# A 3x3 convolution by minimal filtering, and the opening of a scan stage written out for all engines by halves

## The chip, the cores and the metric

The kernel runs on one core of one Trainium2 chip, all in fp32. The metric is the time on the device in microseconds (us). A core has five engines with an instruction queue each: TensorE (PE in the profile; PEld is its weight load), VectorE (DVE), ScalarE (ACT), GpSimd (POOL) and SyncE (SP, which here only issues transfers). An engine works through its own queue in order; between engines, semaphores say when a result is there.

## The reference, cut to what matters

Four layers, each added onto x, each behind a group norm (32 groups of 4 channels); x is 2 images of 128 channels and 56 x 56 points.

```python
# layer 0: agent attention;  layer 1: 3x3 convolution;  layer 2: experts on 2x2 patches;  layer 3: two mambas
x = x + _L0_conv_ref(_gn(x), ...)
x = x + _L1_conv_ref(_gn(x), L1_conv_weight, L1_conv_bias)
x = x + _L2_conv_ref(_gn(x), L2_conv_router_w, L2_conv_w1, L2_conv_w2)
x = x + _L3_conv_ref(_gn(x), ...)

def _L1_conv_ref(x, weight, bias):      # pad 1, stride 1, by FFT in the reference
    ...
    return out + bias[None, :, None, None]

def _mamba(x, in_w, conv_w, conv_b, xproj_w, dt_w, dt_b, Alog, Dp, out_w):
    xi, z = jnp.split(x @ in_w.T, 2, axis=-1)
    xc = jax.nn.silu(conv_b + sum((xp[:, k:k + L, :] * conv_w[:, k] for k in range(K))))
    dt, Bm, Cm = jnp.split(xc @ xproj_w.T, [DT_RANK, DT_RANK + D_STATE], axis=-1)
    dt = jax.nn.softplus(dt @ dt_w.T + dt_b)
    # per row of the image, along its 56 points:
    h = jnp.exp(dt_l[:, :, None] * A) * h + (dt_l * u_l)[:, :, None] * B_l[:, None, :]
    y = jnp.einsum('bds,bs->bd', h, C_l)
    ...
```

The second mamba runs over reversed rows; both results are fused, normalized and added onto x.

## The kernel before, in words

x stays on the chip, channels on partitions (`net.x`, [128, 2, 3136]). An image is worked in seven blocks of 448 points (8 rows of 56). `net.xb(b, k)` is block k of image b, `net.take_stats` its bn_stats; `net.norm_stages` gives the group norm in three stages (bn_aggr; a matmul for group means; a matmul and an inverse root for deviations).

**Attention** (`short_attention`). Fourteen blocks (7 per image), each of 25 steps over the keys. In a step TensorE makes scores (line 617), ScalarE their exponentials (620), VectorE adds them up (`ex_sum`, 625 and 627), and TensorE multiplies by values (635). The order of PE, ScalarE and VectorE is written out (`manual_schedule`), and other work is put into the steps one stage at a time: for the block before (`after`), for the next block (`ahead`), and from a list, `rest`. The denominators (`sum_up`, 655) need VectorE's sums. From the last but one block on, `rest` holds the norm of image 0 for the convolution and its seven `conv.pad` stages: a memset of the edges on GpSimd and a norm on VectorE (line 135) into a padded image of 58 x 58, in the room of `xn0`.

**Convolution** (`Conv3x3`). `loads` brings the weights and transposes the nine taps. `block` makes a block of 8 rows by nine matmuls of 448 columns (line 910), one for each tap, on shifted views of the padded image; one VectorE instruction adds result and bias onto x (917), another takes statistics. Image 0's seven blocks follow the attention, with the seven last stages of the last attention block between them (`tail`). Then comes a verdict over the softmaxes' ranges (`worst`, `bad`, `w_ps`, 830 to 848), the last use of the attention's memory. Image 1 (`convolved(1)`) is done inside `experts.route`: its norm, its pads, its seven blocks; after two of them come the patches of image 0 (`patches(0)`: norm, four normalized quarters, router logits, transposes into DRAM). This part is ordered by the scheduler of the framework. The weights of the mambas (`MambaWeights`) are loaded from ScalarE's queue in the same stretch.

**Experts.** Routing sorts tokens into tiles; 28 tiles run two matmul layers each, with weights streamed by SyncE.

**Mambas** (`mamba_pair`). `arrive(b)` fetches the experts' rows by 14 gathers on GpSimd (`combine`, two for each of seven pieces; line 1200), adds each pair on VectorE (1311), transposes on TensorE (1315), adds onto x (1321), takes statistics, and then the norm of image b. An image block then goes through two halves (ways), f and b. Of a half: `conv` (two matmul groups, m = 0 and 1), `silu` (which loads a ScalarE table for Silu and then the one for exp and log), `low` and `send_low` (projections, through DRAM to B and C), `step`/`error`/`log`/`softplus` (dt, with m = 0 and 1), `weigh` (dt x xc on GpSimd, line 1673, and a memset in dt) and `send_steps` (eight transfers that spread dt and dtu, line 1686, by SyncE). Then 16 units of the scan: `decay` (ScalarE, 1700), `push` (GpSimd, 1711), `scan` (VectorE, 1733), multiplication by C on GpSimd (1739) or VectorE (1742), `collect` (TensorE). There are 28 halves and 448 units.

The order of the scans is written out for all engines: `book(step, stage)` puts a stage at a step of an agenda, 32 steps a block; its `fetch`, which reads the PSUM result, runs a step later. The first block's stages have negative steps. In the opening only ScalarE's order is written out; the others follow the scheduler, and `arrive(1)` comes after the negative steps in the program.

Of the kernel before, what the change touches and what calls it, by code (L numbers as in the profile page):

```python
# [166 lines left out]
def agent_attention(net, wide=None, conv=None):  # L167
# [5 lines left out]
    with ExitStack() as ctx:  # L173
# [48 lines left out]
        def queries(b):  # L222
# [28 lines left out]
            for k in range(NBLK):  # L251
                et = work.tile([2 * agents, 2, BLK], F32, name="et", tag="et", bufs=1)
                e_ps = sc_ps.tile([P, 2, 512], F32, name="e_ps", tag="sc")
                for half in range(2):
# [16 lines left out]
                    en = work.tile(shape, F32, name="a_en", tag="a_en")  # L271
# [137 lines left out]
def short_attention(net, wide, conv):  # L409
# [20 lines left out]
    with ExitStack() as ctx:  # L430
# [35 lines left out]
        taps = conv.loads(one.tile([P, N], F32, name="cw", tag="k1")[:, : 9 * P], bank)  # L466
# [5 lines left out]
        for b in range(NB):  # L472
# [3 lines left out]
            m.va = one.tile([P, len(tiles), P], F32, name=f"va{b}")  # L476
# [59 lines left out]
        def keys(m, k):  # L536
            if k == 0:
                m.k = one.tile([P, N], F32, name=f"k{m.b}", tag=f"k{m.b}")
            cols = slice(k * BLK, (k + 1) * BLK)
            k_ps = bank("k_ps")  # L540
            nc.tensor.matmul(k_ps[:, :BLK], wk, m.xn[:, cols], start=True, stop=True)
            return lambda: nc.scalar.copy(m.k[:, cols], k_ps[:, :BLK])
# [225 lines left out]
        with tc.manual_schedule(engines={E.PE, E.Activation, E.DVE}):  # L768
# [10 lines left out]
            for n, blk in enumerate(blocks):  # L779
                if n == len(blocks) - 2:  # L780
                    pad = one.tile([P, PAD * PAD], F32, name="pad0", tag="xn0")
                    rest = conv.norm(0, banks, "mm")
                    rest += [lambda k=k: conv.pad(0, pad, k) for k in range(NBLK)]
# [36 lines left out]
            tail = [getattr(prev, after[i]) for i in sorted(after)]  # L820
            for k in range(NBLK):
                if k < len(tail) and tail[k]:
                    fetch = tail[k]()
                conv.block(0, k, pad, bank("conv_ps"))
                if k < len(tail) and tail[k] and fetch:
                    fetch()
# [28 lines left out]
class Conv3x3:  # L855


    def __init__(self, net, keep):
        self.net = net
        self.wt = keep.tile([P, 9, P], F32, name="cwt")  # L860
        self.bias = net.column("L1_conv_bias")
        self.norms = {}

    def loads(self, raw, bank):
# [5 lines left out]
        def turn(some):  # L870
            ps = bank("cw_ps")
            for n, k in enumerate(some):
                nc.tensor.transpose(ps[:, n * P : (n + 1) * P], w[:, :, k], net.ident)
            to = self.wt[:, some[0] : some[-1] + 1, :].rearrange("c k f -> c (k f)")
            return lambda: nc.scalar.copy(to, ps[:, : len(some) * P])

        return [lambda some=some: turn(some) for some in (range(0, 4), range(4, 8), range(8, 9))]
# [9 lines left out]
    def pad(self, b, pad, k):  # L887

        nc = self.net.nc
        p3 = pad.rearrange("c (h w) -> c h w", w=PAD)  # L890
        r0 = 1 + k * ROWS
        edges = [p3[:, r0 : r0 + ROWS, 0], p3[:, r0 : r0 + ROWS, PAD - 1]]
        if k == 0:
            edges.append(p3[:, 0, :])
        if k == NBLK - 1:
            edges.append(p3[:, PAD - 1, :])
        for edge in edges:
            nc.gpsimd.memset(edge, 0.0)
        self.net.normed(
            p3[:, r0 : r0 + ROWS, 1 : PAD - 1],  # L900
            self.net.xb(b, k).rearrange("c (h w) -> c h w", w=HW),
            self.norms[b],
        )

    def block(self, b, k, pad, acc):
        net, nc = self.net, self.net.nc
        p3 = pad.rearrange("c (h w) -> c h w", w=PAD)
        for n in range(9):
            i, j = divmod(n, 3)
            nc.tensor.matmul(  # L910
                acc[:, :BLK].rearrange("f (r w) -> f r w", w=HW),
                self.wt[:, n, :],
                p3[:, k * ROWS + i : k * ROWS + i + ROWS, j : j + HW],
                start=n == 0,
                stop=n == 8,
            )
        nc.vector.scalar_tensor_tensor(net.xb(b, k), acc[:, :BLK], self.bias, net.xb(b, k), ALU.add, ALU.add)
        net.take_stats(b, k)
# [6 lines left out]
class PatchExperts:  # L925
# [15 lines left out]
    def route(self, dram, wpool, conv):  # L941
# [9 lines left out]
        with tc.tile_pool(name="l2_route", bufs=1) as one, tc.tile_pool(  # L951
# [116 lines left out]
            for k, _ in enumerate(conv(1)):  # L1068
                if k == 1:
# [230 lines left out]
    def combine(self, b, gathered, bank):  # L1300

        net, nc = self.net, self.net.nc
        half = self.half
        for k in range(self.nt // NB):
# [7 lines left out]

# [5 lines left out]
            r0 = k * (T // half)  # L1318
            for q in range(4):
                xv = self.place(b, q)[:, r0 : r0 + T // half, :]  # L1320
                nc.vector.tensor_tensor(
                    xv, xv, tp[:, q * T : (q + 1) * T].rearrange("c (h w) -> c h w", w=half), ALU.add
                )
            net.take_stats(b, k)
# [102 lines left out]
def mamba_pair(net, out, wts, combine):  # L1427
# [19 lines left out]
    with ExitStack() as ctx:  # L1447
# [20 lines left out]
        def arrive(b):  # L1468

            combine(b, gathered, wide_bank)  # L1470
            mean, rstd = net.group_norm(b, ps, "mm")
# [3 lines left out]
            norms[b] = (both_of[:, 1:2], both_of[:, 0:1])  # L1475

# [96 lines left out]
        class Half:  # L1573
# [97 lines left out]
            def weigh(self):  # L1671
                self.dtu = self.u
                nc.gpsimd.tensor_mul(self.dtu, self.dt, self.xc)

                at = 0 if self.w.d == "f" else HW - 1
                nc.gpsimd.memset(self.dt.rearrange("p m (r t) -> p (m r) t", t=HW)[:, :, at : at + 1], 1e31)

            def send_steps(self, first=False):

                self.dt2 = work.tile([P, 2, 2, BLK], F32, name="dt2", tag="dt2")  # L1680
                self.dtu2 = work.tile([P, 2, 2, BLK], F32, name="dtu2", tag="dtu2")
                for some in (slice(0, 1), slice(1, 2)) if first else (slice(0, 2),):
# [303 lines left out]
```

## Time and profile before

| | us |
|---|---|
| median of three timed runs | 3152.46 (3149.33 to 3153.22) |
| the profiled execution, its own time | 3161.96 |
| its span in the trace | 3160.2 |
| TensorE, VectorE, ScalarE, GpSimd busy | 2864.5, 2200.8, 1752.5, 1411.3 |
| conv 0: first matmul | 884.9 |
| conv 1: first matmul, last eviction | 946.8, 1002.0 |
| first expert matmul | 1050.1 |
| first gather, first scan of the mambas | 1697.6, 1786.25 |

In a row of the timeline: start (us), length (us), engine, line, operation, out<-in with shapes, how many were merged, and in brackets the engine's idle time before it with what ended it. "remote" is a wait whose releaser the trace does not show, "issue" time in which the engine waited for nothing shown. A matmul in fp32 leaves two records, and the ends of matmuls are modelled. Windows give busy time of each engine in a stretch and the granted TensorE clock (1.00 is full).

### The profile page before, as it was taken

How to read it: one execution, taken by the hardware profiler on the slowest of the kernel's cores; microseconds unless marked ns; L12 is line 12 of the kernel's file. 1: busy time of each engine (PE TensorE's matmuls, PEld its weight loads, DVE VectorE, ACT ScalarE, POOL GpSimd, SP SyncE). 2: the span in 40 equal slices, each digit the busy share in tenths (PEclk: the TensorE clock that was granted, in tenths of full speed). 3: DMA queues.
4: the chain of work that ended last, by engine and by line, in shares of the span. 5: the costliest groups of instructions: out<-in, count | busy, mean ns of one | idle time of the engine just before them, and what ended most of it. 6: DMA issues, size and time to landing. Idle time of an engine off the chain costs nothing. (4 is left out here: it accounts for less than half of the span.)

```text
span 3160.2 us, 34597 instructions
## 1 busy us (share of the span) xinstructions
PE 2864.5 (91%) x13024; PEld 1091.8 (35%) x13024; DVE 2200.8 (70%) x1985; ACT 1752.5 (55%) x2618; POOL 1411.3 (45%) x755
## 2 busy tenths in 40 slices
PE   7999999999998899999985689898999899898985
PEld 3333333333344444444442223333233333233321
DVE  5879989988954111111112479999999999999996
ACT  5777887887811011111110467767777767777764
POOL 2000100100000000000003389999999999999995
PEclk9999999999999899999996789998899988999987
DMA  1000000000011878787755434444444444444450
GB/s 53 1 1 1 1 1 1 1 1 1 1 37 41 319 285 319 287 318 287 318 200 165 90 80 86 103 89 102 91 88 90 98 95 95 91 86 99 85 107 7
DMA packets 133525, 333.65 MB, mean 106 GB/s; under 512 B 20228, under 2 KB 90724, under 8 KB 129748
## 3 DMA queue, kind: packets, MB, share of 16 engines
q1 hardware_dynamic: 111744, 304.88, 33.6%
q0 software_dynamic: 5136, 14.70, 1.4%
q10 hardware_dynamic: 16452, 11.61, 1.1%
q8 instruction: 107, 1.75, 0.2%
q14 instruction: 86, 0.70, 0.1%
HBM read 262.56 MB, written 17.20 MB: 89 GB/s over the span
## 5 line engine op out<-in xcount | busy, mean ns | idle before, releaser
L1711 POOL TENSOR_TENSOR dBu<-dtu,Bs 128x896 f32<-128x896 f32 x448 | 923.8, 2090 | 76.1 <-DVE h L1733 60.7
L1733 DVE TENSOR_TENSOR_SCAN h<-dA,dBu 128x896 f32<-128x896 f32 x448 | 878.8, 2007 | 57.5 <-ACT dA L1700 57.2
L620 ACT ACTIVATE ex<-sc 128x896 f32<-128x896 f32 (+1 forms) x700 | 602.7, 917 | 114.0 <-PE sc L617 102.5
L627 DVE TENSOR_TENSOR ex_sum<-ex_sum,ex 128x1792 f32<-128x1792 f32 (+1 forms) x238 | 489.7, 2057 | 35.8 <-ACT ex L620 21.7
L1753 PE MATMUL y<-h,both 128*64 128x448 f32 x1792 | 474.4, 631 | 15.5 <-POOL h L1739 12.9
L617 PE MATMUL sc<-q,k 32*128 32x448 f32 (+1 forms) x2800 | 402.5, 586 | 3.6 <-ACT ex L620 2.9
L1249 PE MATMUL h_ps<-w,xs_c 128*128 128x512 f32 x896 | 392.1, 596 | 10.7 <-issue 9.9
L1700 ACT ACTIVATE dA<-dt,f_A 128x448 f32<-128x448 f32 x448 | 284.5, 637 | 108.9 <-DVE h L1733 76.1
L635 PE MATMUL av<-ex,va 128*32 128x448 f32 (+1 forms) x2800 | 334.3, 552 | 0.1
L1742 DVE TENSOR_TENSOR h<-h,c_ps 128x1792 f32<-128x1792 f32 x154 | 311.3, 2022 | 31.1 <-PE c_ps L1721 16.2
L582 POOL TENSOR_TENSOR a_e<-a_e,a_inv 112x784 f32<-112x784 f32 x14 | 41.6, 2974 | 625.6 <-ACT ex L620 437.2
L1700 ACT ACTIVATE dA<-dt,b_A 128x448 f32<-128x448 f32 x448 | 283.7, 636 | 63.3 <-DVE h L1733 50.4
L1253 DVE TENSOR_TENSOR he<-h_ps,sg 128x512 f32<-128x512 f32 x56 | 38.6, 692 | 397.4 <-PE h_ps L1249 375.0
L1200 POOL DMA_INDIRECT xr<-xd,whom x28 | 28.2, 1005 | 592.7 <-PE xr_ps L1239 489.2
L1739 POOL TENSOR_TENSOR h<-h,Cs 128x1792 f32<-128x1792 f32 x70 | 279.2, 3988 | 2.4 <-DVE h L1733 1.9
L1721 PE MATMUL c_ps<-low,ident 40*64 40x448 f32 x616 | 175.9, 653 | 89.8 <-DVE h L1742 67.6
L1249 PEld LDWEIGHTS h_ps<-w,xs_c 128*128 128x128 f32 x896 | 168.6, 191 | 218.7 <-issue 202.0
L1753 PEld LDWEIGHTS y<-h,both 128*64 128x64 f32 x1792 | 117.9, 152 | 322.6 <-issue 252.9
L617 PEld LDWEIGHTS sc<-q,k 32*128 32x128 f32 (+1 forms) x2800 | 137.7, 181 | 228.8 <-issue 129.5
L1270 PE MATMUL o_ps<-w,ht 128*128 128x512 f32 x448 | 200.0, 599 | 8.0 <-DMA w<-in_L_conv_w_dram 8.0
L1272 ACT ACTIVATE ot<-o_ps,share 128x512 f32<-128x512 f32 x28 | 19.3, 688 | 287.1 <-PE o_ps L1270 287.1
L1252 ACT ACTIVATE sg<-h_ps 128x512 f32<-128x512 f32 x56 | 33.4, 597 | 257.4 <-PE h_ps L1249 257.3
(318 smaller groups left out, 3007.3 us busy)
## 6 DMA issues: line engine op xcount, KB each, us to landing
w<-in_L_conv_w_dram SPq DMA_DIRECT2D x28, 4096.0 KB, 19.4
w<-in_L_conv_w_dram SPq DMA_DIRECT2D x28, 2048.0 KB, 10.2
Bs<-far SPq DMA_DIRECT2D x56, 896.0 KB, 10.5
dtu<-sp_u SPq DMA_DIRECT2D x108, 224.0 KB, 3.9
dt<-dt SPq DMA_DIRECT2D x108, 224.0 KB, 5.2
Cs<-far SPq DMA_DIRECT2D x140, 112.0 KB, 7.4
os<-ot ACTq DMA_DIRECT2D x28, 256.0 KB, 7.8
xd<-xt SPq DMA_DIRECT2D x14, 224.0 KB, 2.7
```

Of the source, the lines that this page charges most:

```text
L617: nc.tensor.matmul(sc[:size, j, :BLK], self.m.k[rows, at : at + size], self.q[rows, :], start=True, stop=True)
L620: nc.scalar.activation(ex[:size, 2 * g : 2 * g + 2, :], sc[:size, :, :BLK], AF.Exp, scale=scale)
L627: nc.vector.tensor_add(self.total[g][:size], self.total[g][:size], ex[:size])
L635: nc.tensor.matmul(self.av[rows, :BLK], self.m.va[:size, i, rows], self.ex[i][:size, h, :], start=i == 0, stop=i == STEPS - 1,)
L1249: nc.tensor.matmul(h_ps, xc[:, q, :], w1[:, q, f0 : f0 + 512], start=q == 0, stop=q == 3)
L1270: nc.tensor.matmul(o_ps, ht[:, i, :], w2[:, i, :], start=i == 0, stop=i == nj - 1)
L1700: nc.scalar.activation(self.dA[u][:, r * BLK : (r + 1) * BLK], self.dt2[:, m, r, :], AF.Exp, scale=self.w.A[:, j, 2 * m + r : 2 * m + r + 1],)
L1711: nc.gpsimd.tensor_tensor(self.dBu[u], self.dtu2[:, m], self.B[:, j, :].unsqueeze(1).to_broadcast(shape), ALU.mult)
L1733: nc.vector.tensor_tensor_scan(hf, af, bf, 0.0, ALU.mult, ALU.add)
L1739: nc.gpsimd.tensor_tensor(h4, h4, c, ALU.mult)
L1742: nc.vector.tensor_tensor(h4, h4, c, ALU.mult)
L1753: nc.tensor.matmul(self.y[r * H : (r + 1) * H, m, :BLK], both, self.hc[j][:, m, r, :], start=False, stop=j == PAIRS - 1)
```

## The change

1. The convolution is done by minimal filtering along the rows, F(2,3): each pair of neighbouring outputs comes from four products (planes) instead of six. The taps k0, k1, k2 of a row become k0, (k0+k1+k2)/2, (k0-k1+k2)/2, k2, made by four GpSimd operations (`mix`). The input becomes four planes of half width, made by four tensor_tensors for each block: on GpSimd for image 0, on VectorE for image 1 (`planes`). The work goes by groups of 16 rows (the last of 8), in two parts, left and right: two planes of three matmuls each. Results are put together from PSUM by VectorE and ScalarE, and by two GpSimd operations (`group`, `rest`).
2. The tail of the attention becomes eight parts with the remaining stages and the three stages of image 1's norm between them. `patches(0)` comes after the first group of image 1 instead of its second block.
3. `combine` and `arrive` become generators: the transposed piece is added onto x one piece later. All five engines' order in the opening is written out: `arrive(0)`, and then the negative steps with pieces of `arrive(1)` between them. `seen`, a small ScalarE copy, stands ahead of the table load.
4. In the first block both convs of a half are booked side by side in two PSUM banks, f's dt is made, weighed (on VectorE) and sent by halves, and dt goes out from ScalarE's queue, dtu from SyncE's. b's convs are booked behind this.

```diff
@@ short_attention
-                    pad = one.tile([P, PAD * PAD], F32, name="pad0", tag="xn0")
+                    planes = [
...
+                        for i, tag in enumerate(("xn0", "k0"))
+                    ]
+                    scratch = one.tile([P, len(tiles), P], F32, name="scratch", tag="va0")
...
-                    rest += [lambda k=k: conv.pad(0, pad, k) for k in range(NBLK)]
+                    rest += [lambda k=k: conv.planes(0, planes, k, scratch, nc.gpsimd) for k in range(NBLK)]
...
+            total, means, deviations = conv.norm(1, banks, "mm")
+            tail = [
+                [prev.divide],
+                [prev.project, prev.measure, prev.root],
+                [prev.normalize],
+                [prev.turn_back, prev.restat, total],
+                [means],
+                [deviations],
+            ]
...
+            for n, (part, ready) in enumerate(parts):
+                for stage in tail[n] if n < len(tail) else ():
+                    do(stage)
+                part()
+                if ready:
+                    ready()
+            end()
@@ class Conv3x3
+    GROUPS = ((0, 16), (16, 16), (32, 16), (48, 8))
...
+    def planes(self, b, planes, k, scratch, engine):
...
+        at = k % 2 * ROWS * PAD
+        p3 = scratch[:, at : at + ROWS * PAD].rearrange("c (h w) -> c h w", w=PAD)
+        nc.gpsimd.memset(p3[:, :, :: PAD - 1], 0.0)
         self.net.normed(
+            p3[:, :, 1 : PAD - 1], self.net.xb(b, k).rearrange("c (h w) -> c h w", w=HW), self.norms[b]
         )
+        even, odd = (p3.rearrange("c h (w two) -> c h two w", two=2)[:, :, i, :] for i in range(2))
...
+                (even[:, :, :half], even[:, :, 1:], ALU.subtract),
+                (odd[:, :, :half], even[:, :, 1:], ALU.add),
+                (even[:, :, 1:], odd[:, :, :half], ALU.subtract),
+                (odd[:, :, :half], odd[:, :, 1:], ALU.subtract),
...
+            engine.tensor_tensor(planes[n // 2][:, n % 2, rows, :], left, right, op)
...
+        def products(two):
+            m = banks("conv_ps")
+            for i in range(2):
+                for row in range(3):
+                    nc.tensor.matmul(
+                        m[:, i, :n],
+                        self.wt[:, row, 2 * two + i, :],
+                        planes[two][:, i, r0 + row : r0 + row + rows, :].rearrange("c h w -> c (h w)"),
...
+        def left():
+            m = products(0)
+            nc.vector.tensor_tensor(x[:, 0], x[:, 0], grid(m[:, 0, :n]), ALU.add)
+            nc.scalar.activation(first, m[:, 1, :n], AF.Identity, bias=self.bias, scale=1.0)
+
+        def right():
+            m = products(1)
+            nc.scalar.copy(second, m[:, 0, :n])
+            nc.vector.tensor_tensor(x[:, 1], x[:, 1], grid(m[:, 1, :n]), ALU.subtract)
+
+        def rest():
+            nc.gpsimd.tensor_tensor(gap, first, second, ALU.subtract)
+            nc.gpsimd.tensor_tensor(first, first, second, ALU.add)
+
+            nc.vector.tensor_tensor(x[:, 1], x[:, 1], grid(gap), ALU.add)
+            nc.vector.tensor_tensor(x[:, 0], x[:, 0], grid(first), ALU.add)
+            for k in range(r0 // ROWS, (r0 + rows) // ROWS):
+                net.take_stats(b, k)
@@ mamba_pair
+            def weigh(self, m=None):
...
+                engine = nc.gpsimd if m is None else nc.vector
+                engine.tensor_mul(self.dtu[:, some], self.dt[:, some], self.xc[:, some])
...
+            def send_steps(self, m=None):
...
+                for to, src, queue in ((self.dtu2, self.dtu, nc.sync), (self.dt2, self.dt, nc.sync if m is None else nc.scalar)):
...
+                book(at + 3, lambda f=f: f.conv(0))
+                book(at + 4, lambda f=f: f.conv(1), tag="c")
+                book(at + 6, lambda f=f: silu(f, None))
+                book(at + 7, f.low)
+                book(at + 9, lambda f=f: f.step(0))
+                book(at + 9, lambda f=f: f.step(1), tag="c", late=1)
+                book(at + 9, f.send_low)
+                for m in range(2):
+                    book(at + 10 + m, lambda f=f, m=m: f.error(m))
+                    book(at + 10 + m, lambda f=f, m=m: f.log(m))
+                    book(at + 11 + m, lambda f=f, m=m: f.softplus(m), tag=("mm", "c")[m])
+                    book(at + 12 + m, lambda f=f, m=m: f.weigh(m))
+                    book(at + 12 + m, lambda f=f, m=m: f.send_steps(m))
...
+                book(at + 17, lambda b=b: b.conv(0))
+                book(at + 17, lambda b=b: b.conv(1), tag="c")
+                book(at + 19, lambda b=b: silu(b, None))
...
-        with tc.manual_schedule(engines={E.Activation}):
-            nc.scalar.preload_act_table_set(EXP_LN)
-            arrive(0)
-            for step in range(min(agenda), 0):
+        with tc.manual_schedule(engines={E.PE, E.Activation, E.DVE, E.Pool, E.SP}):
+            for n, _ in enumerate(arrive(0)):
+                if n == 1:
+
+                    seen = work.tile([P, 1], F32, name="seen", tag="seen", bufs=1)
+                    nc.scalar.copy(seen, net.xb(0, 0)[:, 0:1])
+                    nc.scalar.preload_act_table_set(EXP_LN)
+            second = arrive(1)
+            first = min(agenda)
+            for step in range(first, 0):
                 run(step)
+                for _ in range((0, 0, 0, 0, 2, 1, 2, 1, 2, 0, 0, 0, 0, 0, 1, 1, 1)[step - first] if step - first < 17 else 1):
+                    next(second, None)
                 fetch(step + 1)
-            arrive(1)
+            for _ in second:
+                pass
```

Room sizes and tags change with it (`k` and `cw` 58 x 58, `wt` twelve planes, `a_en` of the fallback one buffer).

## Prediction

> **What bounds the kernel now.** I read the share of each stage first: the busy time of the engines in windows that I cut at the first and last instruction of each stage (the columns are length, then busy time of TensorE, its weight loads, VectorE, ScalarE and GpSimd with the number of instructions, granted clock, DMA share, GB/s).
>
> ```profile
> 700.00:885.00 185.00, 176.56 (x1405) 55.95 (x1401) 165.94 (x148) 141.69 (x176) 11.47 (x5) 0.98 0.00 1
> 885.00:935.00 50.00, 50.00 (x138) 25.59 (x138) 19.70 (x49) 1.81 (x4) 5.47 (x24) 0.97 0.15 49
> 935.00:947.00 12.00, 6.05 (x22) 3.71 (x21) 7.17 (x36) 0.93 (x5) 0.72 (x16) 0.69 0.45 41
> 947.00:1002.00 55.00, 54.98 (x186) 28.92 (x186) 17.24 (x47) 5.11 (x10) 0.00 (x0) 0.98 0.10 30
> 1002.00:1050.00 48.00, 30.07 (x159) 23.48 (x158) 25.67 (x95) 5.56 (x12) 5.10 (x5) 0.67 0.53 194
> 1697.00:1737.00 40.00, 10.99 (x44) 7.67 (x44) 19.34 (x65) 2.97 (x4) 27.61 (x27) 0.50 0.53 150
> 1737.00:1786.00 49.00, 32.23 (x76) 14.26 (x76) 13.69 (x44) 18.89 (x28) 5.26 (x4) 0.78 0.40 85
> 1786.00:3160.00 1374.00, 1207.66 (x4088) 412.47 (x4088) 1258.24 (x866) 966.50 (x1589) 1266.99 (x585) 0.88 0.42 88
> ```
>
> The two convolutions (885 to 935 and 947 to 1002) are TensorE alone, full at full clock, with the others idle: time taken from TensorE there is time of the kernel. Between them lie 12 us in which nobody is full. In the attention's last part TensorE (95%) and VectorE (90%) are both nearly full. The mambas' opening, 1697 to the first scan at 1786, is a chain: no engine is busy in it for more than two thirds. The scans behind it are steady (VectorE and GpSimd 92%), so whatever comes earlier in front of them ends earlier. Likewise 1002 to 1697: routing must end before the experts' first load, and the experts fill TensorE (97%).
>
> The timeline gives a convolution block's price, by its eviction:
>
> ```profile
> 988.51 0.68 DVE L917 SCALAR_TENSOR_TENSOR x<-conv_ps,c_L_conv_bias,x 128x448 f32<-128x448 f32 x1 [5.42 <-PE conv_ps L910]
> 995.27 0.68 DVE L917 SCALAR_TENSOR_TENSOR x<-conv_ps,c_L_conv_bias,x 128x448 f32<-128x448 f32 x1 [5.42 <-PE conv_ps L910]
> ```
>
> 6.76 us for nine matmuls of 448 columns: 0.752 us each.
>
> **Convolution, TensorE.** The pad's nine taps become four planes with three row taps each: 12 matmuls of 448 columns for 16 rows, where there were 18. An image has 42 (3.5 groups) for 63: 21 x 0.752 = 15.8 us off each, 31.6 us in all. The last groups' matmuls have 224 columns; a weight load's 0.19 us still lies beside their 0.19 us passes: nothing.
>
> **Image 0, what the planes cost the attention.** The planes are made in the last but one attention block, where the pads were: the same seven norms on VectorE, and then 28 GpSimd tensor_tensors of 224 columns, their sources strided by two. What a GpSimd operation does to VectorE there:
>
> ```profile
> 800.12 1.96 DVE L627 TENSOR_TENSOR ex_sum<-ex_sum,ex 128x1792 f32<-128x1792 f32 x1
> 800.34 3.09 POOL L582 TENSOR_TENSOR a_e<-a_e,a_inv 112x784 f32<-112x784 f32 x1 [56.11 <-DVE a_inv L581]
> 801.99 1.46 DVE L698 SCALAR_TENSOR_TENSOR ln_t<-ln_mv,ln_rstd 112x4 f32<-112x4 f32 x1
> 803.48 0.16 DVE L699 SCALAR_TENSOR_TENSOR ln_t<-ln_t,ln_rstd 112x4 f32<-112x4 f32 x1
> ```
>
> They take turns. The GpSimd multiplication takes 1.50 us when VectorE is idle and 3.09 here; it ends as the ln_t ends, which took 1.46 instead of 0.16: 1.30 us lost to VectorE for 784 columns. Under x<-x,z (448 columns) an ex_sum takes 2.78 instead of 2.02: 0.76. Both are 1.68 ns a column, so 224 columns cost VectorE 0.38 us, and 28 of them 10.5 us. VectorE's idle times from the first pad (804.9) to the end of the attention (0.76, 0.93, 0.47 and short ones in the timeline) are some 2.9 us, and TensorE's last denominators wait for VectorE already (1.6 us). So 10.5 - 2.9 = 7.6 us come onto the path, most of it before conv 0 starts. The Trainium skill (GPSIMD Engine Reference, Specifications) names the cause: both engines share their SBUF interfaces, and a VectorE instruction with two SBUF inputs contends[...]. It gives no price for a turn. If an operation shut VectorE out for its whole own time (0.19 us fixed and 2.1 ns a column, from 896 columns in 2.09 us and 1792 in 3.99: 0.66 us), it would be 18.5 - 2.9 = 15.6 us, all that conv 0 saves. I take the rows' 7.6; bounds 3 (turns that fall on reciprocals and reductions) and 16. No row has GpSimd with strided sources; on VectorE x<-x,y_ps, strided by two, shows no penalty (0.27 us for 112 columns).
>
> **Conv 0 itself.** Eight parts of six matmuls, 4.5 us each (the last two 2.3), with the rest of the last attention block between them. Per group VectorE has two evictions of 0.68, two additions of 0.63, two statistics of 0.63 (3.9 us in 9.0 of TensorE), ScalarE 2 x 0.53, GpSimd 2 x 1.13. Three PSUM slots let TensorE run ahead: hidden. The statistics' tail grows: copy, GpSimd difference, addition and bn_stats for one eviction and bn_stats: about 1.3 us, in each image. Norm 1 goes from the gap into the tail, hidden.
>
> **The gap.** Norm 1 leaves it, but conv 1's first group needs the planes of three blocks, now on VectorE: a norm 0.44 and four times 0.30 (224 columns at 1.04 ns and about 0.07) are 1.65 us a block, 4.6 us until the left planes of block 2 are there. The verdict (worst, bad, w_ps) still stands before it: in the trace the memsets of the pad wait for w_ps, about 5.4 us after the last matmul. 5.4 + 0.4 + 4.6 = 10.4 and some small work against 12.0: 1 us gained, the longer tail included.
>
> **Conv 1.** TensorE 31.6 + 7.3 (router, transposes of patches) = 38.9 us for 54.7. VectorE now has 11.5 of planes, 13.6 of evictions and statistics, some 5 of turns with GpSimd, 6.8 of patches, 5 of weights: 42 us in a stretch of 46. It is close to the second bound, and ScalarE, which now evicts half of the products, also issues some 30 weight loads at 0.4 to 0.7 us. I take 2 us for both (0 to 8): 13.8 us gained, less 1.3 of tail: 12.5.
>
> **The opening.**
>
> ```profile
> 1724.44 0.34 DVE L100 BATCH_NORM_AGGREGATE gn_mv<-st 128x2 f32<-128x42 f32 x1
> 1727.86 0.16 DVE L107 COPY gn_mean<-gn_ps 128x1 f32<-128x1 f32 x1 [2.95 <-remote]
> 1733.55 0.16 DVE L66 TENSOR_SCALAR ir_v<-gn_ps 128x1 f32<-128x1 f32 x1 [4.79 <-remote]
> 1737.47 0.77 ACT L1493 ACTIVATE pad<-x,norm 128x448 f32<-128x448 f32 x1 [2.02 <-issue]
> 1776.65 2.08 POOL L1673 TENSOR_TENSOR sp_u<-dt,xc 128x896 f32<-128x896 f32 x1 [38.57 <-ACT dt L1669]
> 1781.30 2.45 SPq L1686 DMA_DIRECT2D dt<-dt  x4
> 1784.83 1.32 ACT L1700 ACTIVATE dA<-dt,f_A 128x448 f32<-128x448 f32 x2 [4.25 <-DMA dt<-dt]
> 1786.25 2.02 DVE L1733 TENSOR_TENSOR_SCAN h<-dA,dBu 128x896 f32<-128x896 f32 x1 [4.83 <-ACT dA L1700]
> ```
>
> Gathers are GpSimd's (1.28 us apart) and unchanged; image 0's seventh addition can start at 1718.5. With image 1 behind it, bn_aggr starts at about 1722.3, 2.1 us earlier. The norm takes 12.9 us here, 4.0 in the routing stage; 1.3 of the difference is a table load that the change takes out, 7.7 are two waits whose releaser the trace doesn't show. I leave half of these in: pad at about 1730.8 instead of 1737.5.
> From there: pad 0.8, two convs 4.9 + 3.3, eviction 0.6, table load 1.3, Silu 0.95, low 1.7 + 0.5: low at 1745 (was 1754). But image 1's seven blocks (0.69 + 0.9 + 0.6 on VectorE, 15.5 us) now stand in VectorE's queue ahead of the first error, and their first transposes stand behind both convs on TensorE: the error waits until 1755.5, though its input is ready at 1748.5 (was 1761.8). Then log, the second step (2.3), error, log, copy, and weigh by halves on VectorE 0.62 (GpSimd took 2.1), at 1761.6. ScalarE now issues dt's DMAs itself, 2.4 us a half (SyncE's four took 2.45): both halves landed near 1769.5. Not these release the first decay, but ScalarE's own queue: b's convs follow on TensorE, and silu(b) with two table loads (3.5 us) stands before it. The TensorE clock decides: here 0.50 was granted while TensorE did 11 us of work in 40, and the first four conv matmuls took 4.90, the next 3.31. The skill (TensorE: Matmul & The Clock Gate, Part 1) lets full clock come only after some 3.4 us of steady work. At full clock b's convs take 6.6 us and the first scan comes at 1775.7; half cold 9.8, and 1778.5. I take 1777: 9.2 earlier. The second scan, which waited 3.1 us for the second half's dt, then follows at once: 12.3 us, I take 12 (5 if the unexplained waits return, 18 if they go).
>
> **Sum.** Conv 0: 15.8 - 7.6 = 8.2; gap 1; conv 1: 12.5; opening 12; 33.7 us. The profiled execution took 3161.96 (span 3160.2), 9.5 over the median of the timed runs, 3152.46. Taken from that: 3118.8, say 3119 us. Taps, tile sizes and the fallback's a_en cost nothing here (the taps' four GpSimd operations fall into an early block).
>
> **Rivals.**
> - Twice the price for turns (strided sources), and VectorE the bound of conv 1: conv 0 saves 0, conv 1 only 6; 1 + 6 + 12 = 19 us: 3133. For it: no strided GpSimd row; 42 of 46 us. Against: 1.68 ns a column twice.
> - The opening's chain only re-forms (VectorE's queue, table loads): it saves 3, the sum 25 us: 3128. For it: the error's 7 us of waiting.
> - Turns mostly hidden, and the waits in the norm gone: 15.8 - 3 + 1 + 13 + 18 = 45 us: 3108.
> - The other side, slower: GpSimd's turns in the attention. Without them the change saves 41 us, so they decide from (41 + 2.9)/28 = 1.6 us an operation, four times what the rows give; at 2 us: 3152 + 12 = 3164. Against: even the 784 columns cost 1.30.
> - Most gains hidden anyway, within 0.2% (6 us, what a measurement here can tell from no change): the steady stages behind say no.
>
> **Chances.** Forecast 0.51, first rival 0.17, second 0.11, third 0.13, slower 0.04, no change 0.04. The range 3101 to 3139 reaches over the first three rivals. Faster by over 0.2%: 0.91 (some of the first rival's tail counts as the same), within 0.2% 0.05, slower 0.04.
>
> **What would show it.** 126 conv matmuls become 84, and conv 0 and 1 last 34 and 39 us. Ex_sums of 2.4 us among the planes' steps, and conv 0's start 6 to 9 us later. Conv 1 starts 10 to 12 us after conv 0's last matmul. The first scan comes 77 to 82 us after the first gather (was 88.7), the second right behind it. I am wrong if conv 0 starts over 15 us later, if TensorE in conv 1 waits for VectorE or ScalarE by more than 5 us, or if the error waits for image 1 beyond 1760.

## The result, and the profile after

The changed kernel takes 3128.93 us (median of five, 3122.15 to 3133.36) beside 3152.46 for the kernel before (3149.12 to 3153.22 in the same comparison): ratio 0.9929, 95% interval 0.9913 to 0.9944, or 23.5 us. The forecast was 3119. A later comparison on another chip gave 3123.69 beside 3160.78, ratio 0.9876 (0.9855 to 0.9897), or 37 us. The profiled execution took 3131.49 (span 3129.8), 30.4 less in the span than the one before.

The windows of the changed kernel, cut at the same events (first conv matmul, last one, and so on to the first scan; columns as before; conv 0 and conv 1 are the convolutions of image 0 and image 1):

```profile
700.00:894.50 194.50, 180.70 (x1412) 57.06 (x1408) 171.99 (x148) 142.60 (x178) 49.78 (x38) 0.96 0.00 1
894.50:929.80 35.30, 35.30 (x116) 20.45 (x112) 24.48 (x62) 5.86 (x13) 12.00 (x30) 0.95 0.27 70
929.80:938.50 8.70, 1.30 (x7) 0.85 (x7) 7.52 (x27) 0.56 (x3) 2.11 (x9) 0.64 0.46 54
938.50:982.80 44.30, 43.03 (x158) 24.61 (x158) 26.12 (x72) 8.97 (x19) 9.08 (x10) 0.95 0.11 37
982.80:1034.80 52.00, 32.71 (x167) 25.68 (x166) 29.06 (x114) 6.14 (x14) 6.45 (x7) 0.67 0.49 183
1682.60:1710.90 28.30, 8.10 (x32) 5.73 (x32) 16.07 (x53) 1.88 (x4) 21.83 (x22) 0.51 0.57 162
1710.90:1757.10 46.20, 34.69 (x84) 16.97 (x84) 17.36 (x53) 13.94 (x24) 11.67 (x12) 0.75 0.62 136
1757.10:3129.80 1372.70, 1206.32 (x4092) 411.87 (x4092) 1262.70 (x871) 970.42 (x1594) 1284.97 (x584) 0.89 0.42 88
```

Read the lengths. Conv 0 fell from 50.6 to 35.3 with TensorE still full. Conv 1 fell from 55.2 to 44.3, and TensorE is no longer busy all through it (43.03 of 44.3). The attention in front got longer (conv 0 starts at 894.5 instead of 884.9), and so did routing (52.0 for 48.0). The opening up to the first padded block is 28.3 for 40.0. The scans are the same.

| stage | before | after | difference | forecast |
|---|---|---|---|---|
| start to conv 0's first matmul | 884.9 | 894.5 | +9.6 | +7.6 |
| conv 0 | 50.6 | 35.3 | -15.3 | -15.8 |
| gap to conv 1 | 11.3 | 8.7 | -2.6 | -1 |
| conv 1 | 55.2 | 44.3 | -10.9 | -13.8 |
| routing to the first expert matmul | 48.0 | 52.0 | +4.0 | +1.3 (the tail) |
| experts to the first gather | 647.5 | 647.8 | +0.3 | 0 |
| first gather to first padded block | 40.0 | 28.3 | -11.7 | -6.7 |
| on to the first scan | 48.7 | 46.2 | -2.5 | -2.5 |
| the rest | 1374.0 | 1372.7 | -1.3 | -2.8 |
| span | 3160.2 | 3129.8 | -30.4 | -33.7 |

**What the planes cost the attention.** In the timeline of the changed kernel, GpSimd and VectorE in the last but one block, and this block's last denominators on TensorE; the last line is the same denominators in the kernel before:

```profile
822.15 5.84 POOL L947 TENSOR_TENSOR planes<-scratch 128x224 f32<-128x224 f32 x4
822.36 2.38 DVE L625 TENSOR_TENSOR ex_sum<-ex 128x1792 f32<-128x1792 f32 x1
...
839.66 1.72 PE L655 MATMUL den<-ex_sum,full 128*32 128x448 f32 x8 [5.47 <-DVE ex_sum L627]
...
831.69 0.94 PE L655 MATMUL den<-ex_sum,full 128*32 128x448 f32 x8
```

An ex_sum beside a plane takes 2.38 instead of 2.02: the 0.36 that the forecast had as 0.38. But this is not paid 28 times. VectorE's time in all ex_sums from 700 us to conv 0 (length of the window, busy time, number), and its norms for the convolution (busy time, mean ns, then the idle time before them and what ended it), each before and after:

```profile
700.00:884.90 184.90, 133.38 (x66) 0.98 0.00 1
700.00:894.50 194.50, 137.15 (x66) 0.96 0.00 1
L135 DVE TENSOR_SCALAR pad<-x,gn_mean,gn_rstd 128x448 f32<-128x448 f32 x7 | 3.6, 508 | 0.0
L135 DVE TENSOR_SCALAR scratch<-x,gn_mean,gn_rstd 128x448 f32<-128x448 f32 x7 | 5.5, 790 | 4.1 <-POOL scratch L933 4.1
```

The ex_sums take 3.8 us more, the seven norms themselves 1.9, and the norms now wait 4.1 us for the memset of the edges (line 933). The kernel before has such a memset too, and its norms wait 0.0 for it; now it stands in GpSimd's queue behind the planes of the block before. The three sum to 9.8, beside the 9.6 by which conv 0 starts later. And GpSimd is slow there because it waits in its turn: of its 28 plane operations 15 take 0.56 to 0.72 us, the other 13, which wait out an ex_sum, 2.2 to 2.35. So an ex_sum pays once for the operation that it finds under way, and the operations behind that pay for the ex_sum.

Most of this arrives at one place: the block's last denominators on TensorE, which had no wait in the kernel before, wait 5.47 us for VectorE. The window behind that wait shows a second price:

```profile
839.60:845.60 6.00, 5.94 (x40) 1.47 (x40) 5.13 (x4) 1.73 (x2) 6.00 (x5) 0.67 0.00 0
```

In these 6 us the granted clock is 0.67, and the eight denominators take 1.72 where they take 0.96 after a short wait: some 2 us of TensorE's time. At most 1.7 of it comes onto the path, since the next block's first denominators are 9.6 us later than before and these 8.0. In windows of 1 us the clock is full up to 836, 2 us into the wait, and 0.50 from 837 to 843; it is full again from 844, some 4 us after TensorE's work came back at 839.66. The Trainium skill (TensorE: Matmul & The Clock Gate, Part 1) says that the clock halves after about 3.4 us without work and comes back after about 3.4 us of work; here the fall came somewhat earlier, and the return about as the page has it.

**The opening.** The same instructions as before, in the changed kernel:

```profile
1708.05 0.16 DVE L107 COPY gn_mean<-gn_ps 128x1 f32<-128x1 f32 x1 [0.74 <-PE gn_ps L104]
1709.40 0.16 DVE L66 TENSOR_SCALAR ir_v<-gn_ps 128x1 f32<-128x1 f32 x1 [0.74 <-PE gn_ps L116]
...
1750.23 0.64 ACT L1807 ACTIVATE dA<-dt,f_A 128x448 f32<-128x448 f32 x1 [3.60 <-DMA dtu<-sp_u]
1756.07 0.16 DVE L66 TENSOR_SCALAR ir_v<-gn_ps 128x1 f32<-128x1 f32 x1 [7.38 <-PE gn_ps L116]
1756.26 0.20 ACT L67 ACTIVATE ir_t<-ir_v 128x1 f32<-128x1 f32 x1 [5.39 <-DVE ir_v L66]
1756.37 0.62 ACT L1807 ACTIVATE dA<-dt,f_A 128x448 f32<-128x448 f32 x1
1757.09 2.02 DVE L1840 TENSOR_TENSOR_SCAN h<-dA,dBu 128x896 f32<-128x896 f32 x1 [0.86 <-ACT dA L1807]
1759.03 1.91 DVE L69 TENSOR_TENSOR ir_t<-ir_v,gn_rstd 128x1 f32<-128x1 f32 x1
1763.38 5.84 DVE L1840 TENSOR_TENSOR_SCAN h<-dA,dBu 128x896 f32<-128x896 f32 x3
```

Image 0's norm no longer waits (0.74 for 2.95 and 4.79). But between the first decay (1750.23) and the second (1756.37) ScalarE stands 5.39 us at `ir_t`: image 1's norm, whose matmul on TensorE is queued behind b's convs. The same norm stands on VectorE between the first scan and the second, where an operation on one column takes 1.91 us beside GpSimd's pushes. The second scan comes 6.3 us after the first (5.1 in the kernel before), where the forecast had 2.

### The profile page after: what moved, and what is told of

It is laid out like the page before. It is cut to its first block, busy times and chain, and to the rows that moved or that the text cites. A ratio compares the mean times of both kernels' runs of the same rounds, so it can differ in the third digit from the quotient of the medians.

```text
span 3129.8 us, 34601 instructions
## 1 busy us (share of the span) xinstructions
PE 2836.3 (91%) x12964; PEld 1082.0 (35%) x12964; DVE 2229.0 (71%) x2033; ACT 1758.0 (56%) x2634; POOL 1495.6 (48%) x793
## 5 line engine op out<-in xcount | busy, mean ns | idle before, releaser
L1818 POOL TENSOR_TENSOR dBu<-dtu,Bs 128x896 f32<-128x896 f32 x448 | 944.9, 2142 | 54.9 <-DVE h L1840 45.4
L627 DVE TENSOR_TENSOR ex_sum<-ex_sum,ex 128x1792 f32<-128x1792 f32 (+1 forms) x238 | 492.5, 2069 | 35.3 <-ACT ex L620 21.3
## 6 DMA issues: line engine op xcount, KB each, us to landing
Bs<-far SPq DMA_DIRECT2D x56, 896.0 KB, 10.7
```

What stands on the lines that cost most here:

```text
L627: nc.vector.tensor_add(self.total[g][:size], self.total[g][:size], ex[:size])
L1818: nc.gpsimd.tensor_tensor(self.dBu[u], self.dtu2[:, m], self.B[:, j, :].unsqueeze(1).to_broadcast(shape), ALU.mult)
```

## The experiments

My theory after the result: TensorE's saving comes as computed; part is given back by GpSimd's turns in the attention and by VectorE's work that conv 1's planes push into routing; the rest is the opening, of whose profiled gain I took 7 us to be waits of one execution. The experiments ran in three jobs, each on a chip of its own, where the kernel before took 3160.2, 3160.8 and 3151.0 us.

**The kernel before, profiled again.**

> The kernel before, profiled a second time. Theory: the two waits of 2.95 and 4.79 us in the opening's norm belong to that one execution; this span lies within 4 us of 3152, and the stretch from the first gather to the first padded block is some 32 us. Rival: they belong to the kernel; the span is 3160 again, the stretch 40 us, and then the 7 us by which the profiles differ more than the timed runs lie elsewhere.

The timeline at the same place:

```profile
1725.42 0.16 DVE L107 COPY gn_mean<-gn_ps 128x1 f32<-128x1 f32 x1 [3.18 <-remote]
1730.45 0.16 DVE L66 TENSOR_SCALAR ir_v<-gn_ps 128x1 f32<-128x1 f32 x1 [4.12 <-remote]
```

The rival held: span 3158.5, waits of 7.3 us again, and 39.2 us from the first gather to the padded block. The waits belong to the kernel, and the change removes them.

**Each part alone.** The diff's hunks of the convolution, or of `combine`, `arrive`, `weigh`, `send_steps` and the bookings, on the kernel before.

> The convolution's part of the change alone, with the opening of before. Theory: up to the first gather the two profiles differ by 14.9 us, all of it the convolution's; so 15 us faster than before, 3137.5. Rival: the two parts meet somewhere (the opening's order was written around what the scheduler does with the convolution's weights), and this gives less than 10.

3143.18 beside 3160.19: ratio 0.9943 (0.9930 to 0.9957), 17 us. Its profile starts conv 0 at 893.6, and its opening waits 6.23 us at `ir_v`, like before.

> The opening's part alone, with the convolution of before. Theory: the remainder of the timed gain, 23.5 - 14.9 = 8.6 us, since 7 of the 15.5 us that the profiles show were waits of one execution: 3144. Rival: 15.5 us, 3137, and the convolution's part then gives only 8.

3144.84 beside 3160.19: ratio 0.9954 (0.9941 to 0.9968), 15.4 us, with 28.7 us from the gather to the padded block. So the rival was right on the opening (15.5), and the theory on the convolution (15).

> The changed kernel unchanged, beside the others of this job. Theory (the parts add up, and the first comparison fell on a faster run of the kernel before): 18 + 14.5 = 32.5 us faster than before. Rival: the parts meet somewhere, and it is 22.4 us again, as in the first comparison. Conv 0 starts near 894.5.

3123.69 beside 3160.78: 37 us, by its interval 32.6 to 45.8, where the parts measured one by one give 32.4. By this comparison they take nothing from each other. By the first one they would, 9 us of 32.4; there the kernel before was 8 us faster than in this job, the changed kernel 5 us slower. The parts' gains taken off 3160.2 give 3127.8, which lies between the changed kernel's two medians, 3123.7 and 3128.9; it is the kernel before that differs most.

**Image 1's norm moved ahead** (the changed kernel with one line different):

```
-for _ in range((0, 0, 0, 0, 2, 1, 2, 1, 2, 0, 0, 0, 0, 0, 1, 1, 1)[step - first] if step - first < 17 else 1):
+for _ in range((0, 0, 0, 0, 2, 1, 2, 1, 2, 2, 2)[step - first] if step - first < 11 else 1):
```

> The changed kernel with image 1's norm moved from behind the opening's last steps into VectorE's idle times between f's error and weigh stages, ahead of b's convs on TensorE. Theory: in the changed kernel that norm stands on ScalarE between the first and second decay and on VectorE between the first and second scan, behind b's convs and GpSimd's pushes; moved, the first scan comes at 1752.7 instead of 1757.1, the second at 1757 instead of 1763.4; 5 to 6.5 us faster than the changed kernel, 3123. Rival: something else is late next by the same time (the second push, the landing of dtu), and it gives 0 to 2 us, 3128.

In its timeline:

```profile
1738.90 0.16 DVE L69 TENSOR_TENSOR ir_t<-ir_v,gn_rstd 128x1 f32<-128x1 f32 x1 [0.50 <-ACT gn_rstd L68]
...
1749.43 2.02 DVE L1840 TENSOR_TENSOR_SCAN h<-dA,dBu 128x896 f32<-128x896 f32 x1 [5.21 <-POOL dBu L1818]
...
1753.57 5.85 DVE L1840 TENSOR_TENSOR_SCAN h<-dA,dBu 128x896 f32<-128x896 f32 x3 [2.11 <-ACT dA L1807]
```

The norm's operations take 0.16 each, where VectorE had time and GpSimd did nothing. From the padded block to the second scan it is 46.6 us instead of 52.4: 5.8, as the theory had it (the stretches count; this execution was 4 us ahead already when the opening began). What is late next is the push of dtu, then the second decay. The time is 3115.23 beside 3160.19, ratio 0.9864 (0.9849 to 0.9880). Its span is shorter than the changed kernel's by more than this: the scans behind were 9 us shorter, all of it after the twelfth. From there to the end the kernels with this norm ahead take 1319.0, 1319.1, 1323.3 and 1328.0 us in their profiles, the changed kernel 1329.6 and 1330.3, and its variants without this edit 1326.2 to 1327.9. Whether part of that belongs to the edit stays open, so I don't count it.

**The planes on GpSimd twice.**

```
+            for _ in range(2 if b == 0 else 1):
-            engine.tensor_tensor(planes[n // 2][:, n % 2, rows, :], left, right, op)
+                engine.tensor_tensor(planes[n // 2][:, n % 2, rows, :], left, right, op)
```

> Each of image 0's 28 plane operations on GpSimd is done twice, with the same result. Theory (VectorE loses some 0.36 us to each operation in a stretch where it is the bound, and TensorE waits for it): conv 0 starts another 28 x 0.36 = 10 us later than 894.5, at 904 to 905. Rival (the 9.6 us by which conv 0 starts later are VectorE's waits for edges in GpSimd's queue, or a cost of the stage's form): 2 to 4 us later, 897.

Conv 0 starts at 905.8, 11.3 later, as the theory forecast in number (0.40 us for each added operation). Its mechanism fell. The same two groups as above, in this run:

```profile
700.00:905.80 205.80, 137.49 (x66) 0.94 0.00 1
L135 DVE TENSOR_SCALAR scratch<-x,gn_mean,gn_rstd 128x448 f32<-128x448 f32 x7 | 5.5, 783 | 14.7 <-POOL scratch L933 14.7
```

With 28 operations more on GpSimd, VectorE's ex_sums together take 0.3 us longer, and its norms no longer than before. What grew is the norms' wait for the edges in GpSimd's queue, from 4.1 to 14.7: 10.6 of the 11.3. This is the first half of the rival, at a size that it did not expect. The denominators' wait grew with it, from 5.47 to 14.34. The time is 3137.80, 14.1 more than the changed kernel's in the same job.

**The planes dealt out.**

```
-                if n == len(blocks) - 2:
+                if n == NBLK + 1:
...
+                    share = [conv.norm(0, banks, "mm"), [], [], [], [], []]
+                    for k, at in enumerate((0, 1, 2, 3, 4, 4, 5)):
+                        share[at].append(lambda k=k: conv.planes(0, planes, k, scratch, nc.gpsimd))
+                if n > NBLK:
+                    rest += share[n - NBLK - 1]
```

> Image 0's norm and planes begin when image 0 is complete, in the ninth attention block, and are dealt out over six blocks (1, 1, 1, 1, 2, 1) instead of all in the last but one. Theory: a block has some 5 us in which VectorE waits, and seven planes a few us each fit into them: conv 0 starts near 886 instead of 894.5, 8 us faster than the changed kernel. Rival: VectorE is the bound in every attention block, and each pays for its own planes: conv 0 starts at 893 to 895, no gain.

Conv 0 starts at 890.6, 4 us earlier, half of what I expected; the time is 3120.79 beside the changed kernel's 3123.69 in the same job, and their ranges overlap. In this run the norms wait for no memset (0, where it was 4.1) and take 3.8 us; the ex_sums take 3.3 more than in the kernel before. So what dealing out gained is the wait in GpSimd's queue, and the turns stayed. The distance between two blocks' reciprocals of the denominators tells why it is not more. It is 58.6 us in an undisturbed block. The kernel before takes 66.3 in the last but one: the three stages of the norm and the pads cost 7.7 there, which I had not seen. Dealt out, the ninth block (norm and one plane step) takes 66.5, and each plane step alone 0.6 to 0.7 more than 58.6. The last but one block takes 74.8 in the changed kernel and 60.6 here. So a block has no 5 us of slack, but about 1; the norm costs its 7 wherever it stands.

**Three edits together, planes on GpSimd or on VectorE.** Image 1's norm ahead, planes dealt out, and `if k < 2:` ahead of the edges' memset; then the same with `nc.vector` for the planes.

> Three edits together: image 1's norm moved ahead, image 0's planes dealt out over six attention blocks on GpSimd, and the two scratch halves' edge columns set to zero once instead of for each block. Theory (VectorE's waits for edges in GpSimd's queue are part of the 6 us that dealing out left): conv 0 starts at 886 to 888 instead of 890.6, and conv 1, whose planes waited for the edges too, takes 1 us less; with 6 us from the norm 12 us faster than the changed kernel. Rival: what is left are turns, 28 x 0.4 less idle time, wherever they stand: 890, and 10 us.

Conv 0 at 890.5 and conv 1 44.2: beside the planes dealt out alone (890.6 and 44.1) the memsets cost nothing, so the rival was right here. That does not clear them in the changed kernel, since dealing out alone had already brought the norms' wait for them to 0. The changed kernel with this memset edit alone was not run. The time is 3116.27 beside 3150.97, ratio 0.9882 (0.9867 to 0.9898).

> The same as the run before, but image 0's planes are made by VectorE itself (224 columns, 0.31 us each) instead of GpSimd. If a GpSimd operation costs VectorE 0.36 to 0.40 us, VectorE does better to do them itself: conv 0 starts 1 to 2.5 us earlier than with GpSimd. If turns were hidden where the planes are dealt out, it starts later, by up to 28 x 0.31 = 8.7 us.

Conv 0 at 896.0, 5.5 later than with GpSimd; a plane step costs a block 1.6 us. The 28 operations take VectorE 0.41 us each, 11.4 in all, and conv 0 starts 11.1 later than in the kernel before; with GpSimd it is 5.6. 3126.66, ratio 0.9927 (0.9914 to 0.9941), 10.4 us more than with GpSimd; the part of it beyond the 5.5 lies mostly behind the second scan, where profiles vary by as much. VectorE has no room here: GpSimd's turns are the cheaper of the two. The Trainium skill (GPSIMD Engine Reference, Engine selection) puts elementwise work on VectorE, since GpSimd is about half as fast at it; for a stretch that VectorE bounds, this pair says the opposite.

**The weights' copies on ScalarE.** `nc.scalar.copy` in place of VectorE's copies of the transposed weights in `MambaWeights`.

> The transposed weights of the mambas are copied out of PSUM by ScalarE instead of VectorE (31 copies). Theory: routing is 3 to 4 us longer in the changed kernel because VectorE, busy with planes in conv 1, does this work between routing's serial steps; with the copies gone routing takes 48 us again (from conv 1's end to the first expert matmul 45.7 instead of 48.6) and conv 1 1 us less: 3 to 4 us faster than the changed kernel. Rival: routing is longer by its own tail (the last group's evictions, additions and statistics), and nothing changes.

Conv 1 is 2.1 us shorter (42.2), but the gap is 0.8 and routing 0.6 longer: the same total, 3124.23 beside 3123.69. My theory on routing fell. What is left of it is the tail, in the changed kernel's timeline after the last conv matmul (982.8):

```profile
983.50 0.66 POOL L991 TENSOR_TENSOR scratch<-scratch 128x224 f32<-128x224 f32 x1 [1.81 <-ACT scratch L987]
...
986.29 0.33 DVE L100 BATCH_NORM_AGGREGATE gn_mv<-st 128x2 f32<-128x42 f32 x1
```

The aggregation starts 3.5 us after the last matmul (1.6 before): 1.9 of routing's 4. The other 2 I have not traced to an instruction. The windows have 167 matmul records and 114 VectorE instructions in routing where the kernel before has 159 and 95: more of the weights' work stands there now, but that it costs these 2 us is not shown.

**What made image 0's norm wait.** The kernel before with GpSimd's order written out too:

```
-        with tc.manual_schedule(engines={E.Activation}):
+        with tc.manual_schedule(engines={E.Activation, E.Pool}):
```

> The kernel before with one thing different: GpSimd's order is written out in the opening as ScalarE's is, so image 1's gathers, additions and transposes come behind the opening's other steps instead of among them. The question is where the waits of 7 us in image 0's norm come from (TensorE's result is modelled as ready 3 to 6 us before VectorE goes on). If image 1's work among it is the cause: from the first gather to the first padded block 28 to 30 us, as in the kernels with the whole order written out, instead of 39 to 40. If the norm waits for itself (ScalarE's table load, the matmul's own end): 36 to 39. What comes behind the scans' start may be later, since image 1 now stands there as one piece.

```profile
1720.97 0.16 DVE L107 COPY gn_mean<-gn_ps 128x1 f32<-128x1 f32 x1 [0.68 <-PE gn_ps L104]
1722.25 0.16 DVE L66 TENSOR_SCALAR ir_v<-gn_ps 128x1 f32<-128x1 f32 x1 [0.68 <-PE gn_ps L116]
```

Without image 1's gathers, additions and transposes among it the norm waits 0.68 twice, and it is 29.9 us to the padded block: the first theory. Which of the three holds TensorE's result back was not tried. Image 1 now stands as one piece ahead of the scans, the first of which comes 74.0 us after the padded block instead of 48.8: 3173.82 beside 3150.97, ratio 1.0072 (1.0056 to 1.0087). So it is not enough to put image 1 away; it has to go into the idle times, as the change does it.

**One queue for dt and dtu** (with image 1's norm ahead):

```
-                for to, src, queue in ((self.dtu2, self.dtu, nc.sync), (self.dt2, self.dt, nc.sync if m is None else nc.scalar)):
+                for to, src, queue in ((self.dtu2, self.dtu, nc.sync), (self.dt2, self.dt, nc.sync)):
```

> The changed kernel with image 1's norm moved ahead (as in the run before), and dt sent by SyncE's queue too: one queue for all sixteen transfers of a half-block instead of two. Theory: SyncE's issues take 0.6 us each, so that dt's first half lands some 3 us later (the first decay at 1747 instead of 1744), and the second half's dtu and dt some 2 us later; the first scan waits for dtu and the push and stays, the second comes 1 to 3 us later than with two queues. Rival: ScalarE's 2.4 us of issues per half were in the way of its own decays, and one queue gives the same or 1 us.

The first scan comes 45.7 us after the padded block instead of 42.5, which I had not expected, and the second 47.6 instead of 46.6: the second queue is worth 1 us where it counts. 3115.47 beside 3150.97, ratio 0.9896 (0.9878 to 0.9915).

## Why the prediction was right or wrong

The sign held, and so did the mechanism of the convolution's matmuls and of the opening, but not that of the attention's price; of 33.7 us the profiles show 30.4, the comparisons 23.5 and 37. Step by step:

- **Conv 0, TensorE** (15.8): 15.3. The count of matmuls times 0.752 was right.
- **Turns in the attention** (7.6): 9.6, of which 1.1 stood in the first three blocks, before any plane, and 8.5 in the last but one. The number is near, but by luck: the mechanism was wrong. I had VectorE pay 0.38 for each of 28 operations, 10.5 in all, and hide 2.9. An ex_sum does lose 0.36 beside a plane, but all of them together lost 3.8, and 28 operations more cost them 0.3. The rest is 1.9 in the norms and 4.1 of their waits for the edges' memset behind the planes in GpSimd's queue, a term that I had put at nothing. I also left out how it arrives: one wait of 5.47 us on TensorE, and the slow clock behind it.
- **The gap** (1): 2.6. I had conv 1 wait for the planes of three blocks; the first taps need only two (TensorE started 2.75 us after the first memset, not 4.6). A wait for the third block's planes does not show in conv 1: TensorE is busy from its start to 954.5.
- **Conv 1 and its tail** (13.8 - 1.3 = 12.5): 10.9 - 4.0 = 6.9. This is the term that was most mis-sized. I gave 2 us for VectorE and ScalarE together. The tail was 1.9 for 1.3, and routing another 2. In conv 1 itself the trace shows a slow start, and TensorE waiting for the quarters of image 0's patches, which VectorE normalizes (line 135) with no idle time of its own; the last line is the kernel before:

```profile
938.50:942.00 3.50, 3.49 (x5) 1.83 (x6) 3.41 (x11) 0.23 (x1) 0.48 (x2) 0.50 0.00 0
...
955.74 2.71 PE L1098 MATMUL l_ps<-xq,rw 128*32 128x392 f32 x12 [1.26 <-DVE xq L135]
...
961.92 1.52 PE L1017 MATMUL l_ps<-xq,rw 128*32 128x392 f32 x16
```

  The sixteen router records come as the quarters come, twelve and later four, and take 4.2 us where the kernel before had them in one piece of 1.5; with the 1.26 of idle time before them that is 4 us. The slow clock at the start of conv 1 (0.50 in the first 3.5 us; it was 0.59 there before) adds some 0.6 to what it cost already. With VectorE's copies of the weights gone to ScalarE, conv 1 was 2.1 us shorter.
- **The opening** (12): 15.5. I left half of the two waits in; all of them went. The padded block came 5 us earlier than I had it, and the first scan 74.4 us after the first gather instead of 79.4, so what lies between was right in sum. In its parts it was not: I said that silu(b) stands ahead of the first decay, and that the second scan follows at once. The one that stands there is image 1's norm, 5.4 us on ScalarE and 4 on VectorE; it stood in the diff's tuple (the last three ones), and I had not followed where its three stages fall on each queue.
- **The base.** I took the sum from 3161.96 and the median from elsewhere: 9.5 us were put down to one execution. Sixteen timed runs in two of the jobs took 3156 to 3169 (in the third 3148 to 3155), and the part I had called unexplained was in every profile of this kernel's order. From the profile itself the sum gives 3128.3; the changed kernel took 3128.9 and 3123.7. That the sum is 3 us from the profiles' 30.4 is luck in part too: conv 1 with its tail fell short by 5.6 and the attention by 2.0, the opening and the gap gave 3.5 and 1.6 more.

What stays open: why the kernel before takes 3151 to 3152 us in two comparisons and 3160 in two others, when the changed one varies by 5. No execution of 3152 was profiled. And which instruction of image 1 held TensorE's result back.

The best version found is the changed kernel with image 1's norm ahead: 3115 to 3116 in the three kernels that have it and make planes on GpSimd, where the changed kernel took 3124 and 3129. They were not timed in one job with it; what shows a gain is the 5.8 us in the stretch.

## What to carry to other kernels

When an order is written out for all engines, follow every small stage on every queue, not only the chain that was meant: three stages of a norm on one column cost more than the transfers that the order was made for. Where a slower engine works beside one that bounds the stretch, look at its queue as well as at the turns: here a memset of 0.12 us, queued behind the slower engine's work, cost the bounding engine 4.1 us, about as much as its turns, and 14.7 when that work was doubled. Then look where the delay lands: a long wait of TensorE also costs it the clock. When a run doubles a cost and the total fits the theory, check in the trace that the doubled term is the one that grew. A profiled execution that is longer than the timed runs is no reason to discount its waits; profile again first.

## What the runs showed of the hardware

- Beside GpSimd's 224-column operations a 1792-column addition of VectorE takes 2.38 us instead of 2.02, but the loss does not grow with their number: 66 additions took 133.4 us without them, 137.2 with 28 of them, 137.5 with 56. Of the 28 GpSimd operations, 13 waited out an addition and took 2.2 to 2.35 us, the others 0.56 to 0.72.
- An operation of VectorE on a single column takes 1.91 and 2.04 us under GpSimd's 896-column multiplications (2.1 each), and 0.16 with GpSimd idle: its time is nearly the whole length of one of them.
- A result of TensorE can reach VectorE 3 to 6 us after its modelled end (2.95 and 4.79 in the first profile of the kernel before, 3.18 and 4.12 in the second, 6.23 with the convolution's part alone), with nothing in the trace to show why; with other work moved away it takes 0.7.
- TensorE's granted clock fell from 1.00 to 0.50 some 2.5 us into a wait of 5.47, and was full again some 4 us after work came back.
